# Strassen–Winograd block products of an attention kernel: from seven sums out of PSUM per block to five, with the weights' right half as first columns

## The chip, the cores and the metric

The kernel runs on one core of one Trainium2 chip. The metric is the device time of one execution in microseconds (us). The runs of the kernel before gave 1417.74, 1419.90 and 1419.27 us, median 1419.27 us. The engines are named as in the profile: PE (TensorE, matrix products), PEld (its weight loads), DVE (VectorE), ACT (ScalarE), POOL (GpSimd) and SP (SyncE, which issues nearly all DMAs here).

## The reference

There are 64 batches. `x` is 64 x 256 x 512, the context `c` is 64 x 256 x 384, all in fp32.

```python
text_p  = einsum('bld,dh->blh', x, W_text)  + b_text      # 512 -> 512
audio_p = einsum('bsd,dh->bsh', c, W_audio) + b_audio     # 384 -> 512
Q = layer_norm(text_p, g1, beta1);  K = layer_norm(audio_p, g2, beta2);  V = audio_p
alpha = softmax(einsum('blh,bsh->bls', Q, K) / sqrt(512))
h = einsum('bls,bsh->blh', alpha, V)
out = layer_norm(einsum('blh,hk->blk', h, W_out) + b_out + x, g_out, beta_out)
```

Since a softmax row sums to one, the kernel folds `W_audio` and `W_out` into one matrix `wao` and their biases into `bao`, and computes `alpha @ c @ wao + bao`.

## The kernel before

The order of the work is written out by hand: each engine runs its instructions in the order of the program text, and an instruction waits on semaphores for what it needs from the other engines. Tiles come from rotating pools. Of the 8 PSUM banks, six serve the pool `p_pj` (tag "pj"), two the pool `p_at` (scores, context, transposes). A new tile of a pool takes the bank of the tile six (or two) allocations earlier, and waits until that one has been read.

Three matrix products per batch are done by blocks: `q` (x times `W_text`), `k` (c times `W_audio`) and `y` (context times `wao`). Each has 256 rows and 512 columns of output, cut in 2 x 2 quarters of 128 rows by 256 columns, and is made of seven block products numbered 1 to 7 in place of eight (the Strassen–Winograd scheme). POOL adds up the operands beforehand (`weight_sums` and `weights_of_three` once per weight, `sum_x`, L304 to L307, and `sum_c`, L319 to L322, once per batch). A block product is one quarter of 128 x 256 fp32, half a PSUM bank. The method `products(...)` (L465 to L474) takes one bank for the one or two product numbers it is given and issues their matmuls (L472). The profile shows each fp32 matmul as two PE instructions, each called a pass here. One block of q has 28 passes (4 for each product), one of k or y has 22 (2 for products 1, 6 and 7, 4 for the rest).

The method `leave(n)` (L476 to L497, all instructions under L483) adds product n into the rows `qr`, `kr` or `yr` in SBUF, one DVE instruction for each number. Products 1, 6 and 7 go into two quarters (128 x 512, the product read twice by a broadcast), products 2, 5, 3 and 4 into one quarter (128 x 256). So there are seven DVE instructions for each block, and `rows` of the first 128 rows are complete after product 3, those of the second after product 4.

The program has a head (L743 to L853), a loop over 62 batches (L856 to L946) and an end (L949 to L1029).

- One pass of the loop holds on PE: scores of batch b (16 passes, L511), the q block of batch b+2 (28), the context of batch b-1 (12, L577), the k block of batch b+2 (22), and the y block of batch b-1 (22): 100 passes. On DVE it holds, in this order, the last three sums of an earlier y block, transposes of e, x and c squares (L91), the row maxima (L521), the q sums with the reciprocals (L538) between the first and the second of them, the transposes of q and k (L91, L439), the output's scaling (L694, L703), the k sums and the first four y sums.
- After its sums each q and k block goes this way: ACT squares the rows (L380), POOL makes the inverse deviation (L341, L343), ACT scales (L408), SP stores to DRAM (L418) and fetches squares of 32 x 32 in the next pass (L88), DVE transposes, ACT applies gamma and beta (L446), and the scores use the result.
- In the head, the first block product set of batch 1 is interleaved with other work. The lines that matter for q of batch 1 are, in program order:

```python
    part = bias_parts()                     # DVE, L231 and L233: four instructions
    q[1] = Blocks("q", 1, xs.pop(1), wt_blocks, bt_sb)
    q[1].products(1, 2)
    q[1].leave(1)
    q[0].turn()                             # DVE, L91
    q[0].affine(g1_sb, be1_sb)
    q[1].products(6, 5)
    q[1].leave(6)
```

- In the end, the y block of batch 61 (`last.o`) is interleaved likewise: `products(1, 2)`, the transpose of q of batch 63, `leave(1)`, `products(4)`, the transpose of k, `products(6, 5)`, and so on. It is followed on PE by the context of batch 62 and the scores of batch 63, and then by a chain of DVE, ACT and POOL work to the last store.

Of the kernel before, what the change touches and what calls it, by code (L numbers as in the profile page):

```python
# [9 lines left out]
F32 = mybir.dt.float32  # L10
# [5 lines left out]
P = 128  # L16
# [6 lines left out]
def kernel(  # L23
# [57 lines left out]
    p_pj = ctx.enter_context(tc.tile_pool(name="p_pj", bufs=6, space=PSUM))  # L81
# [24 lines left out]
    def load_squares(b):  # L106
        load_c(b)
        load_x(b)

    def load_rows(b):  # L110
        x_sb = xin.tile([P, LT, D], F32, tag="x", name=f"x_{b}")
        c_sb = cin.tile([P, ST, DA], F32, tag="c", name=f"c_{b}")
        nc.sync.dma_start(x_sb, x[b].rearrange("(t p) d -> p t d", p=P))
        nc.sync.dma_start(c_sb, c[b].rearrange("(t p) d -> p t d", p=P))
        return x_sb, c_sb
# [79 lines left out]
    class RowTurn:  # L195


        def __init__(self, rows_sb, chunks, name):
            self.rows, self.chunks = rows_sb, chunks
            tag = "yr" if chunks == DC else "kT"  # L200
            self.ar = work.tile([P, 2, chunks, P], F32, tag=tag, name=f"{name}r")
            self.T = work.tile([P, chunks, 2 * P], F32, tag=name, name=f"{name}_0")
# [81 lines left out]
    H2 = H // 2  # L284

    def weight_sums(w_sb, n, name):

        w = [[w_sb[:, j * n : (j + 1) * n, k * H2 : (k + 1) * H2] for k in (0, 1)] for j in (0, 1)]
        t = const.tile([P, 4, n, H2], F32, tag=name, name=name)
        add = nc.gpsimd.tensor_tensor  # L290
        add(t[:, 0], w[0][1], w[0][0], ALU.subtract)
        add(t[:, 1], w[1][1], t[:, 0], ALU.subtract)
        add(t[:, 2], w[1][1], w[0][1], ALU.subtract)  # L293
        add(t[:, 3], w[1][0], t[:, 1], ALU.subtract)
        ws = {1: w[0][0], 2: w[1][0], 3: w[1][1], 4: t[:, 3], 5: t[:, 0], 6: t[:, 1], 7: t[:, 2]}
        return {p: [ap[:, k, :] for k in range(n)] for p, ap in ws.items()}
# [31 lines left out]
    def weights_of_three(w_sb, name):  # L328

        ws = weight_sums(w_sb, 1, name)  # L330
        for n, k2 in ((2, 0), (3, 1), (5, 1), (4, 0)):
            ws[n].append(w_sb[:, 2, k2 * H2 : (k2 + 1) * H2])
        return ws

    def rstd_of(var, n, total=False):
# [118 lines left out]
    class Blocks(Projection):  # L454
# [3 lines left out]

        def __init__(self, name, b, sides, weights, bias):
            super().__init__(name, b, None, None, bias, None, 2)
            self.sides, self.weights = sides, weights

        def products(self, *ns):  # L465

            bank = p_pj.tile([P, 2, H2], F32, tag="pj", name=f"ps_{self.name}")
            for j, n in enumerate(ns):
                self.ps[n] = bank[:, j : j + 1, :]
                pairs = list(zip(self.sides[n], self.weights[n]))  # L470
                for i, (side, w) in enumerate(pairs):
                    nc.tensor.matmul(  # L472
                        bank[:, j, :], lhsT=side, rhs=w, start=(i == 0), stop=(i == len(pairs) - 1)
                    )  # L474

        def leave(self, n):  # L476

            both = self.ps.pop(n)
            one = both[:, 0, :]
            both = both.broadcast_to([P, 2, H2])  # L480
            c1, c2 = self.rows[:, 0, :], self.rows[:, 1, :]
            wide = lambda ap: ap.rearrange("p (k h) -> p k h", k=2)
            add = lambda o, i0, i1: nc.vector.tensor_tensor(o, i0, i1, ALU.add)  # L483
            if n == 1:
                add(wide(c1), both, wide(self.bias))
            elif n == 6:
                add(wide(c2), both, wide(c1))
            elif n == 2:
                add(c1[:, :H2], one, c1[:, :H2])
            elif n == 5:  # L490
                add(c2[:, H2:], one, c2[:, H2:])
            elif n == 3:
                add(c1[:, H2:], one, c2[:, H2:])
            elif n == 7:
                add(wide(c2), both, wide(c2))
            elif n == 4:
                add(c2[:, :H2], one, c2[:, :H2])  # L497

    class Attention:
        def __init__(self, b):  # L500
# [227 lines left out]
    def turn_next(b):  # L728
        xT[b] = turn_x(b)
        xs[b] = sum_x(xT.pop(b))  # L730
        cT[b] = turn_c(b)
        cs[b] = sum_c(cT.pop(b))
# [7 lines left out]
    q, k, xT, cT, rows = {}, {}, {}, {}, {0: (x_0, c_0)}  # L740
# [19 lines left out]
    k[0].evict(0)  # L760
    centre(wa_sb, mean_wa, AC)
    wa_blocks = weights_of_three(wa_sb, "wasum")
    for chunks in ([0, 1], [2, 3]):
        for t in range(LT):
# [15 lines left out]
    k[0].fetch()  # L780
    load_c(2)
    wt_blocks = weight_sums(wt_sb, DC // 2, "wtsum")
    q[0].evict(0)
    q[0].evict(1)
# [6 lines left out]
    q[0].fetch()  # L791
    xT[1] = turn_x(1)
    k[1] = Blocks("k", 1, cs.pop(1), wa_blocks, ba_sb)
    k[1].products(1, 2)
    k[1].leave(1)
    k[1].products(6, 5)
    k[1].leave(6)
    k[1].leave(2)
    k[1].leave(5)
    k[1].products(7, 3)  # L800
    k[1].leave(3)
    k[1].leave(7)
    k[1].products(4)
    k[1].leave(4)
    k[1].square()
    k[1].scales()
    xs = {1: sum_x(xT[1])}
# [21 lines left out]
    q[0].affine(g1_sb, be1_sb)  # L829
    q[1].products(6, 5)  # L830
    q[1].leave(6)
    q[1].leave(2)
    q[1].leave(5)
    q[1].products(7, 3)
    q[1].leave(3)
    q[1].leave(7)
    q[1].products(4)
    q[1].leave(4)
    q[1].square()
    q[1].scales()  # L840
    xT[2] = turn_x(2)
# [4 lines left out]
    fold_evict(2)  # L846
    bao_sb = fold_bias(part)
    wao_blocks = weights_of_three(wao_sb, "waosum")
    q[1].normalise()
    q[1].store()  # L850
# [4 lines left out]
    done = last = None  # L855
    for b in range(B - 2):  # L856
        three = b + 3 < B
        at = Attention(b)
        at.scores()
        if done:  # L860
            done.o.leave(3)
            done.o.leave(7)
            done.o.leave(4)
            done.add_x()
        if last:
            last.turn_e()
        if three and b:
            turn_next(b + 3)
        at.maxima()
        at.exponentials()  # L870
        if not b:
            k[1].turn()
        q2 = q[b + 2] = Blocks("q", b + 2, xs.pop(b + 2), wt_blocks, bt_sb)
        q2.products(1, 2)
        q2.leave(1)
        at.reciprocals()
        at.divide_e()
        if not b:
            k[1].affine(g2_sb, be2_sb)
        if b:  # L880
            q[b + 1].fetch()
            k[b + 1].fetch()
        at.store_e()
        if b + 4 < B:
            load_squares(b + 4)
        at.fetch_e()
        rows[b + 1] = load_rows(b + 1)
        if done:
            done.statistics()
        q2.products(6, 5)  # L890
        q2.leave(6)
        q2.leave(2)
        q2.leave(5)
        q2.products(7, 3)
        q2.leave(3)
        q2.leave(7)
        q2.products(4)
        q2.leave(4)
        q2.square()
        q2.scales()  # L900
        q[b + 1].turn()
        if not b:
            turn_next(3)
        if done:
            done.shift(0)
            done.shift(1)
        if last:
            last.context()
        q[b + 1].affine(g1_sb, be1_sb)
        if b:  # L910
            k[b + 1].turn()
            k[b + 1].affine(g2_sb, be2_sb)
        if done:
            done.settle(0)
            done.settle(1)
            done.store()
        q2.normalise()
        q2.store()
        if last:
            last.start_products()  # L920
        k2 = k[b + 2] = Blocks("k", b + 2, cs.pop(b + 2), wa_blocks, ba_sb)
        k2.products(1, 2)
        k2.leave(1)
        k2.products(6, 5)
        k2.leave(6)
        k2.leave(2)
        k2.leave(5)
        k2.products(7, 3)
        k2.leave(3)
        k2.leave(7)  # L930
        k2.products(4)
        k2.leave(4)
        k2.square()
        k2.scales()
        k2.normalise()
        k2.store()
        if last:
            last.o.products(1, 2)
            last.o.leave(1)
            last.o.products(6, 5)  # L940
            last.o.leave(6)
            last.o.leave(2)
            last.o.leave(5)
            last.o.products(7, 3)
            last.o.products(4)
        done, last = last, at  # L946


# [2 lines left out]
    k[B - 1].fetch()  # L951
    rows[B - 1] = load_rows(B - 1)
    at.scores()
    done.o.leave(3)
    done.o.leave(7)
    done.o.leave(4)
    done.add_x()
    add_bias(B - 2)
    last.turn_e()
# [16 lines left out]
    k[B - 1].turn()  # L976
    last.o.products(6, 5)
    last.o.leave(6)
    k[B - 1].affine(g2_sb, be2_sb)
    done.settle(0)  # L980
    last.o.leave(2)
    last.o.leave(5)
    last.o.products(7, 3)
    last.o.leave(3)
    last.o.leave(7)
    last.o.leave(4)
    last.add_x()
    at.context()
    done.settle(1)
# [72 lines left out]
```

## Time and profile before

| | |
|---|---|
| runs, median (lowest to highest) | 1419.27 us (1417.74 to 1419.90) |
| the profiled execution's own time | 1418.87 us |
| its span, first to last instruction | 1417.1 us |
| PE busy | 1404.4 us (99%), 6441 instructions |
| DVE busy | 1273.0 us (90%), 2134 instructions |
| ACT busy | 931.8 us (66%) |
| POOL busy | 878.0 us (62%) |
| granted PE clock, mean | 0.999 |

A line of the groups reads: line, engine, operation, output tile <- input tiles, shapes, count, then busy us in total and mean ns of one, then the idle time just before them with what ended it. The chain of waits is followed back from the last instruction: its pieces are the work or waits that set the end. A timeline line reads: start, us, engine, line, operation, tiles, count, and in brackets the idle time before with what ended it.

### The profile page before, as it was taken

Reading aid. Unit: us, or ns where it says so; the run is one execution under the profiler, and the core shown is the slowest. Engines: PE = TensorE matmul, PEld = TensorE weight load, DVE = VectorE, ACT = ScalarE, POOL = GpSimd, SP = SyncE. Lnnn points to the kernel's source line nnn. Section 1 sums busy time; section 2 is a strip of 40 time slices with the busy share of each in tenths; the row PEclk is TensorE's granted clock in tenths of the full one; section 3 lists DMA queues with packets and bytes.
Section 4 is the critical chain, followed back from the end, with each engine's and each line's share of the span. In section 5 each row is a group of like instructions: output and inputs, shape, how many; then the busy total and the mean of one; then the engine's idle time right before and its main releaser. Section 6 shows DMA issues by size and latency. Waiting matters only on the chain.

```text
span 1417.1 us, 23332 instructions
## 1 busy us (share of the span) xinstructions
PE 1404.4 (99%) x6441; PEld 1220.4 (86%) x6441; DVE 1273.0 (90%) x2134; ACT 931.8 (66%) x2293; POOL 878.0 (62%) x1295
## 2 busy tenths in 40 slices
PE   9999999999999999999999999999999999999997
PEld 5888888888888888888888888888888888888885
DVE  5789999999998999999999999999999999999988
ACT  4666676676676676765766766767667667667662
POOL 4556656666666666575566666665765666666645
PEclk9999999999999999999999999999999999999999
DMA  8898887888887788888878878887888788788763
GB/s 203 227 244 238 240 243 214 238 240 221 235 234 232 227 224 244 237 223 235 243 216 238 240 216 239 231 235 228 228 239 239 220 238 240 218 238 233 220 191 118
DMA packets 450583, 322.61 MB, mean 228 GB/s; under 512 B 154901, under 2 KB 382997, under 8 KB 450453
## 3 DMA queue, kind: packets, MB, share of 16 engines
q1 hardware_dynamic: 450356, 320.98, 79.9%
q8 instruction: 53, 0.87, 0.3%
q14 instruction: 78, 0.63, 0.2%
q10 hardware_dynamic: 96, 0.13, 0.0%
HBM read 204.09 MB, written 116.92 MB: 227 GB/s over the span
## 4 chain that ended last, share of the span: by engine, by line
PE 96%; DMA 1%; POOL 1%; DVE 1%; SPq 0%; issue 0%; ACT 0%; POOLq 0%; DVEq 0%; ACTq 0%
PE ps_q L472 27%; PE ps_y L472 21%; PE ps_k L472 21%; PE ps_sc L511 16%; PE ps_z L577 11%; DMA wt<-in_L_xattn_W_text_dram 1%; DMA xq<-in_x_dram 1%; POOL rstd L343 0%; PE ps_wao L245 0%; DVE st L267 0%; SPq L150 0%; POOL ve L341 0%; DVE y L632 0%; DVE y L698 0%; POOL wtsum L293 0%
## 5 line engine op out<-in xcount | busy, mean ns | idle before, releaser
L341 POOL TENSOR_SCALAR ve<-var 128x2 f32<-128x2 f32 x126 | 44.5, 353 | 305.9 <-ACT junk L380 305.9
L511 PE MATMUL ps_sc<-kT,qT 128*128 128x256 f32 x1024 | 231.5, 379 | 0.0
L528 ACT ACTIVATE e<-ps_sc,nmx 128x256 f32<-128x256 f32 x128 | 59.5, 469 | 246.4 <-DVE nmx L521 246.4
L483 DVE TENSOR_TENSOR qr<-ps_q,qr 128x512 f32<-128x512 f32 x378 | 188.0, 511 | 35.7 <-PE ps_q L472 24.0
L511 PEld LDWEIGHTS ps_sc<-kT,qT 128*128 128x128 f32 x1024 | 194.6, 190 | 26.9 <-ACT qT L446 0.2
L483 DVE TENSOR_TENSOR kr<-ps_k,kr 128x512 f32<-128x512 f32 x378 | 188.1, 511 | 24.3 <-PE ps_y L472 0.5
L483 DVE TENSOR_TENSOR yr<-ps_y,yr 128x512 f32<-128x512 f32 x372 | 185.1, 511 | 23.4
L593 POOL TENSOR_TENSOR yr<-yr,x 128x512 f32<-128x512 f32 x124 | 157.2, 1278 | 57.1 <-DVE yr L483 57.0
L577 PE MATMUL ps_z<-eT,c 128*128 128x256 f32 x768 | 176.5, 379 | 0.1
L472 PE MATMUL ps_q<-wtsum,xsum 128*128 128x256 f32 x756 | 173.6, 379 | 0.6 <-POOL xsum L305 0.6
L343 POOL TENSOR_TENSOR rstd<-ve,nhalf 128x2 f32<-128x2 f32 (+1 forms) x194 | 159.3, 821 | 16.2
L472 PE MATMUL ps_k<-wa,cT 128*128 128x256 f32 x630 | 166.8, 379 | 0.0
L472 PE MATMUL ps_y<-wao,zT 128*128 128x256 f32 x620 | 164.2, 379 | 0.0
L577 PEld LDWEIGHTS ps_z<-eT,c 128*128 128x128 f32 x768 | 145.8, 190 | 20.7 <-ACT e L528 0.5
L472 PEld LDWEIGHTS ps_q<-wtsum,xsum 128*128 128x128 f32 x756 | 143.6, 190 | 20.5 <-POOL xsum L305 1.0
L380 ACT ACTIVATE junk<-kr 128x512 f32<-128x512 f32 x126 | 79.3, 630 | 98.9 <-DVE kr L483 98.9
L446 ACT ACTIVATE qT<-qT,columns 128x256 f32<-128x256 f32 x256 | 132.8, 592 | 6.6 <-DVE qT L91 6.6
L472 PEld LDWEIGHTS ps_k<-wa,cT 128*128 128x128 f32 x630 | 119.6, 190 | 16.2
L446 ACT ACTIVATE kT<-kT,columns 128x256 f32<-128x256 f32 x256 | 132.1, 588 | 1.1 <-DVE kT L91 1.0
L472 PEld LDWEIGHTS ps_y<-wao,zT 128*128 128x128 f32 x620 | 117.7, 190 | 16.0
L408 ACT ACTIVATE kr<-kr,rstd 128x512 f32<-128x512 f32 x126 | 84.1, 714 | 70.7 <-POOL rstd L343 70.7
L703 DVE SCALAR_TENSOR_TENSOR yr<-yr,rstd,beo 128x512 f32<-128x512 f32 x124 | 127.5, 1066 | 0.6 <-POOL rstd L343 0.6
(150 smaller groups left out, 2945.9 us busy)
## 6 DMA issues: line engine op xcount, KB each, us to landing
kd<-kr SPq DMA_DIRECT2D x64, 512.0 KB, 3.1
kq<-kd SPq DMA_DIRECT2D x256, 128.0 KB, 3.4
qd<-qr SPq DMA_DIRECT2D x64, 512.0 KB, 5.5
qq<-qd SPq DMA_DIRECT2D x256, 128.0 KB, 3.3
xq<-in_x_dram SPq DMA_DIRECT2D x252, 128.0 KB, 2.9
x<-in_x_dram SPq DMA_DIRECT2D x63, 512.0 KB, 4.1
out_dram<-yr SPq DMA_DIRECT2D x62, 512.0 KB, 5.0
cq<-in_ctx_dram SPq DMA_DIRECT2D x252, 96.0 KB, 2.5
```

Source lines behind the costliest of these rows:

```text
L341: nc.gpsimd.tensor_scalar(ve, var, EPS, None, ALU.add)
L343: nc.gpsimd.tensor_tensor(r, ve, nhalf[:, :n], ALU.pow)
L380: nc.scalar.activation(junk, self.rows[:, t, :], AF.Square, scale=1.0 / math.sqrt(H), accum_out=self.var[:, t : t + 1],)
L408: nc.scalar.mul(row, row, self.r[t])
L446: nc.scalar.activation(self.T[:, k, :], self.T[:, k, :], AF.Identity, bias=bet[:, k : k + 1], scale=gam[:, k : k + 1],)
L472: nc.tensor.matmul(bank[:, j, :], lhsT=side, rhs=w, start=(i == 0), stop=(i == len(pairs) - 1))
L483: add = lambda o, i0, i1: nc.vector.tensor_tensor(o, i0, i1, ALU.add)
L511: nc.tensor.matmul(self.sc[:, t, :], lhsT=self.qT[:, k, bass.ts(t, P)], rhs=self.kT[:, k, :], start=(k == 0), stop=(k == HC - 1),)
L528: nc.scalar.activation(self.e[:, t, :], self.sc[:, t, :], AF.Exp, bias=self.nmx[:, t : t + 1], accum_out=self.den[:, t : t + 1],)
L577: nc.tensor.matmul(ps[:, j, :], lhsT=self.c_sb[:, s, bass.ts(lo + j, P)], rhs=self.eT[:, s, :], start=(s == 0), stop=(s == ST - 1),)
L593: nc.gpsimd.tensor_tensor(self.y[:, t, :], self.y[:, t, :], self.xb[:, t, :], ALU.add)
L703: nc.vector.scalar_tensor_tensor(self.y[:, t, :], self.y[:, t, :], self.r[t], beo_sb, ALU.mult, ALU.add)
```

## The change

The two column halves of the weights change roles: what the block scheme calls the first columns is now the right half of the weight. With that, products 2 and 5 belong to two quarters that are neighbours in the rows, and products 3 and 4 to the first and the last quarter, at one stride. Each of these two pairs shares a PSUM bank, and leaves it in one DVE instruction over 128 x 2 x 256. So a block has five sums (1, 6, 2+5, 3+4, 7), not seven. The banks are now by group, (1, 6), (2, 5), (3, 4) and (7), and `products` takes the bank of a group when the first of its products is issued. The order of the products in the loop becomes 1, 6, 2, 5, 3, 4, 7; the q block's sum of product 6 moves ahead of the reciprocals. In the head, `q[1].products(1, 2)` keeps its place, and so does `products(6, 5)` behind `q[1].leave(1)`; in the end the y block keeps `products(1, 2)`, `products(4)` and `products(6, 5)` in theirs. The instructions of ACT, POOL and SP keep their number, kind and order.

```diff
     def weight_sums(w_sb, n, name):
-        w = [[w_sb[:, j * n : (j + 1) * n, k * H2 : (k + 1) * H2] for k in (0, 1)] for j in (0, 1)]
+        w = [[w_sb[:, j * n : (j + 1) * n, k * H2 : (k + 1) * H2] for k in (1, 0)] for j in (0, 1)]
...
-            ws[n].append(w_sb[:, 2, k2 * H2 : (k2 + 1) * H2])
+            ws[n].append(w_sb[:, 2, (1 - k2) * H2 : (2 - k2) * H2])
...
         def products(self, *ns):
-            bank = p_pj.tile([P, 2, H2], F32, tag="pj", name=f"ps_{self.name}")
-            for j, n in enumerate(ns):
-                self.ps[n] = bank[:, j : j + 1, :]
+            for n in ns:
+                group = next(g for g in ((1, 6), (2, 5), (3, 4), (7,)) if n in g)
+                if group not in self.banks:
+                    self.banks[group] = p_pj.tile([P, 2, H2], F32, tag="pj", name=f"ps_{self.name}")
+                place = self.banks[group][:, group.index(n), :]
...
-        def leave(self, n):
...
+        def leave(self, *ns):
+            bank = self.banks[(1, 6) if ns[0] in (1, 6) else ns]
+            quarters = self.rows.rearrange("p t (k h) -> p (t k) h", k=2)
+            c1, c2 = quarters[:, :2], quarters[:, 2:]
...
+            elif ns == (2, 5):
+                add(quarters[:, 1:3], bank, quarters[:, 1:3])
+            elif ns == (3, 4):
+                add(quarters[:, 0:4:3], bank, c2)
...
         if not b:
             k[1].turn()
         q2 = q[b + 2] = Blocks("q", b + 2, xs.pop(b + 2), wt_blocks, bt_sb)
-        q2.products(1, 2)
+        q2.products(1, 6)
         q2.leave(1)
+        q2.leave(6)
         at.reciprocals()
...
-        q2.products(6, 5)
-        q2.leave(6)
-        q2.leave(2)
-        q2.leave(5)
-        q2.products(7, 3)
-        q2.leave(3)
+        q2.products(2, 5)
+        q2.leave(2, 5)
+        q2.products(3, 4)
+        q2.leave(3, 4)
+        q2.products(7)
         q2.leave(7)
-        q2.products(4)
-        q2.leave(4)
...
     q[1].products(6, 5)
     q[1].leave(6)
-    q[1].leave(2)
-    q[1].leave(5)
-    q[1].products(7, 3)
-    q[1].leave(3)
+    q[1].leave(2, 5)
+    q[1].products(3, 4)
+    q[1].leave(3, 4)
+    q[1].products(7)
     q[1].leave(7)
-    q[1].products(4)
-    q[1].leave(4)
...
     last.o.products(6, 5)
     last.o.leave(6)
+    last.o.leave(2, 5)
     k[B - 1].affine(g2_sb, be2_sb)
     done.settle(0)
-    last.o.leave(2)
-    last.o.leave(5)
-    last.o.products(7, 3)
-    last.o.leave(3)
+    last.o.products(3)
+    last.o.leave(3, 4)
+    last.o.products(7)
     last.o.leave(7)
-    last.o.leave(4)
```

## The prediction

> **What bounds the kernel now.** I read four views: the busy shares on the page, the waits by engine, the chain of waits, and the order of DVE's work where PE stops.
>
> Waits of PE, with engine and line waited for, us in total, times, longest:
>
> ```profile
> PE ps_ones L193 <- POOL ones L122: 1.5, 1, 1.5
> PE ps_y L472 <- DVE kr L483: 1.4, 1, 1.4
> PE ps_q L472 <- POOL xsum L305: 0.6, 1, 0.6
> ```
>
> PE is 99% busy, and these are its longest waits, each of which occurs once. None belongs to a steady loop pass. From there on PE runs its 100 passes in 21.58 us, pass after pass, without a gap (712.46 to 734.04 us between the starts of two q blocks: 215.8 ns each). The loop goes at PE's pace, and time can only come or go where PE waits: in the head and in the end.
>
> The chain of waits in the head (start, us, work):
>
> ```profile
> 36.17 0.74 POOL xsum L305
> 36.92 0.04 issue
> 36.96 4.58 PE ps_q L472 x20
> 41.54 3.43 PE ps_wao L245 x8
> ...
> 76.92 2.60 PE ps_y L472 x12
> 79.52 0.04 issue
> 79.56 0.70 DVE kr L483
> 80.27 0.02 issue
> 80.29 0.44 DVE kr L483
> 80.72 0.14 issue
> 80.86 2.40 PE ps_y L472 x10
> 83.25 3.45 PE ps_sc L511 x16
> ```
>
> At 36.96 the matmuls of q[1]'s product 6 start, as soon as POOL has their operand. All later pieces are PE's, back to back, until 79.52. There the third bank of the first y block is the first bank of the k block before it, and PE waits until DVE's third k sum has read it (80.29 to 80.72).
>
> DVE's timeline at the places where a first sum lies between two products, in the head and in the end:
>
> ```profile
> 36.31 0.88 DVE L231 TENSOR_SCALAR part<-wo,columns 128x512 f32<-128x512 f32 x1
> 37.22 3.02 DVE L233 SCALAR_TENSOR_TENSOR part<-wo,columns,part 128x512 f32<-128x512 f32 x3
> 40.16 0.68 DVE L483 TENSOR_TENSOR qr<-ps_q,bt 128x512 f32<-128x512 f32 x1
> ...
> 1385.81 1.25 DVE L91 STREAM_TRANSPOSE qT<-qq 128x1024 f32<-128x1024 f32 x1 [0.41 <-DMA qq<-qd]
> 1386.98 0.65 DVE L483 TENSOR_TENSOR yr<-ps_y,bao 128x512 f32<-128x512 f32 x1
> ```
>
> The sum of product 1 runs late in both: at 40.16, behind the bias parts, and at 1386.98, behind a transpose.
>
> **Fewer sums.** Groups of DVE by form (count, then busy us and mean ns):
>
> ```profile
> L483 DVE TENSOR_TENSOR qr<-ps_q,qr 128x256 f32<-128x256 f32 x252 | 100.9, 421 | 23.5 <-PE ps_q L472 14.2
> L483 DVE TENSOR_TENSOR qr<-ps_q,qr 128x512 f32<-128x512 f32 x126 | 87.1, 691 | 12.2 <-PE ps_q L472 9.8
> ```
>
> Four sums of 421 ns become two of 691 ns (taking the row for 512 elements; the stride of 3+4 has no row): 1684 - 1382 = 302 ns less per block. With 63 q, 63 k and 62 y blocks that is 57 us of DVE. On the path it is worth nothing: what hides it is PE's unbroken row of passes, 21.58 us against 19.8 us of DVE in a pass. If that cover were gone, up to 57 us would show.
>
> **The order 1, 6, 2, 5, 3, 4, 7 and the moved sum.** The operands of product 6 are there: zsum's second step ends at 723.5, and y needs it at 726.3. Nothing is paid. In q, the sum of product 6 (0.69) now stands ahead of the reciprocals, where DVE idled 0.49 us for ACT. The reciprocal comes some 0.25 us later, and behind it ACT's division, SP's store of e and SP's loads queued after it. e returns for a transpose in the next pass that does not wait for DMA. Price nothing; if that cover is gone, 0.25 x 62 = 15 us.
>
> **The wait at 79.52 gets shorter or goes.** The first k bank now holds 1 and 6 and is free after the second sum, 0.46 us earlier (80.25, not 80.71). The wait cost 83.25 - 76.92 - 4.75 = 1.58 us (a y block without it takes 4.75).
>
> **A new wait in the head.** q[1]'s products 1 and 6 now share a bank, and between them stands `leave(1)`. The changed program's list of waits says it: the first matmul of product 6 waits for the DVE instruction that sums product 1. Before, 6 lay in another bank. ACT, POOL and SP are unchanged, and DVE reaches that sum by the same instructions, so it ends at 40.84 again. With the 0.14 us from a sum's end to PE's start (80.72 to 80.86), product 6 starts at 40.98, not at 36.96: +4.02 us. Queued behind it on PE is all the rest, and the chain from 36.96 to 79.52 has no slack. A lower bound: two of the three L233 instructions took 1.10 us beside POOL, the third 0.75; were all like the third, +3.3.
>
> How much comes back? PE now reaches the place of the old wait at 83.54. The k sums there follow a chain of row maxima, sums, scaling, store and fetch. Part of it moves with PE, part was waiting for DMA. Following it, I get the second k sum done between 80.6 and 82.5: the old wait is gone, -1.58. If all moved by 4.02, only the 0.46 came back. So the head costs 4.02 - 1.58 = 2.44, at most 3.56. Later batches repeat the loop without a wait.
>
> **A new wait in the end.** The same occurs in y of batch 61: product 6 started at 1387.11, and the sum of product 1 ends at 1387.63; +0.14 for the start and +0.1 for the restart (after a wait the second pass comes 0.3 us after the first, not 0.2): +0.76. The transpose ahead of that sum waited 0.41 us for DMA; the k and q sums before its fetch now end some 0.4 us earlier, which may remove as much: +0.35. I take 0.5. It is on the path: the last scores follow on PE without a gap, and the row maxima at 1395.94 wait for them. The shorter y sums between gain nothing there.
>
> **Sum.** The profiled execution took 1418.87 us (span 1417.1 and 1.8 around it): 1418.87 + 2.44 + 0.5 = 1421.8. The median of the runs lies 0.40 above the profiled execution: 1422.2. That is +0.21%. About 0.2%, 2.84 us, is what a measurement of this kernel can tell from no change, so "slower" and "same" meet nearly at my number.
>
> **A rule against it.** PE's last pass before the new wait starts at 36.00, so it stands idle for about 4.7 us. In this trace PE waits of 1.35 us leave the clock at 1.00, and after the last matmul at the end of the program (1409.4) the windows show 1.00 until 1414.5 and 0.59 for 1414.5 to 1415: it falls 5.2 us after. By these rows 4.7 us is just under it. If the clock did fall: at the start, passes of 128 columns stand 213 ns apart from 1.5 to 4.9 us and 110 ns after, 3.3 us at half rate, a loss of at most 1.7.
>
> The Trainium skill, "TensorE: Matmul & The Clock Gate" (Part 1), states that the clock falls to half after an idle window of some 3.4 us, windows that run free of the program. By that rule the idle stretch can catch a whole window in some executions and not in others; with the loss above, such an execution would take 1423.9 us.
>
> **Rivals.**
> - *The clock falls in the new gap*: +1.1 to +1.7 more, 1423.3 to 1423.9. For: the length of the gap. Against: the 5.2 us at the end.
> - *Not slower: the old wait and the head's other chains take the new wait up.* What bound PE at 79.52 was a chain through DMA and DVE, so a head that is late on PE could find room behind it. This decides only if PE has over 4 us of waits after 41 us; the trace shows 1.58. What speaks for it is that batch 1's own fetches were waiting for DMA. Result: 1418.0 to 1419.7.
> - *DVE's 57 us show*, if the loop hung on DVE: 1362 to 1375. Against: DVE idles each pass, PE never.
> - *A wait in each loop pass*, by the moved sum or a bank: from 0.1 us a pass it is +6, with 0.25 it is +15: 1428 to 1437. Against: banks are free over 1.5 us ahead (k's second sum ends at 726.6, y's third bank is needed at 728.43).
>
> **Chances.** Forecast (1421.0 to 1423.0) 0.62; clock 0.20; taken up 0.08; DVE 0.03; loop wait 0.07. The forecast splits at 1422.1, the bound: 0.33 slower, 0.29 same. The clock case is slower but for 0.01, the loop wait slower, "taken up" same, DVE faster but for 0.01. Sum: slower 0.59, same 0.39, faster 0.02. The range reaches from 1420.0 (between "taken up" and the forecast, with the lower bounds of +3.3 and +0.35) to 1424.8 (the clock case with the upper bound of the wait in the end and part of the 3.56).
>
> **What would show it.** Right: a PE wait at `ps_q` for DVE `qr` of about 4.6 us near 41 us, a short one at `ps_y` for DVE `yr` near 1390 us, none for `kr`; DVE busy about 1216 us; a loop pass still 21.58 us; the page's clock slices near 41 us tell whether it fell. Wrong: a loop pass other than 21.58 us, or a product 6 that starts before its neighbour's sum has ended.

## The result, and the profile after

| | before | after |
|---|---|---|
| runs, median (lowest to highest) | 1419.27 us (1417.74 to 1421.16), 9 runs | 1423.60 us (1423.23 to 1425.29), 9 runs |
| the profiled execution and its span | 1418.87, 1417.1 us | 1425.29, 1423.5 us |
| mean granted PE clock | 0.999 | 0.996 |
| DVE busy | 1273.0 us | 1232.9 us |

The ratio is 1.0031 [1.0023, 1.0040]: slower by 0.3%, and the predicted 1422.2 us was 1.4 us short. The profiled execution after is the slowest of its nine, 1.7 us above their median; its head is already 0.9 us late at the first block product on PE, ahead of which no PE instruction was changed (first pass of k[1] at 23.69 us against 22.76, of q[1] at 35.42 against 34.49).

PE's waits after, in the columns of the prediction:

```profile
PE ps_q L478 <- DVE qr L490: 4.7, 1, 4.7
PE ps_ones L193 <- POOL ones L122: 1.5, 1, 1.5
```

The forecast wait is there, the old one on `kr` is gone. The chain of waits after, in the head and around the first y block:

```profile
37.31 0.87 DVE part L231
...
41.22 0.61 DVE qr L490
41.83 0.14 issue
41.96 7.34 PE ps_q L478 x20
...
84.67 4.75 PE ps_y L478 x22
```

The chain now runs through the bias parts and the sum of product 1, and the y block has its bare 4.75 us. But the 20 passes of q[1] behind the wait take 7.34 us where they took 4.58. The windows view shows why (start and end of the stretch, its length, busy us of PE, PEld, DVE, ACT and POOL with their instructions, granted clock, DMA share, GB/s):

```profile
33.95:37.36 3.41, 3.36 (x13) 1.96 (x11) 1.53 (x5) 2.45 (x8) 1.82 (x4) 1.00 0.91 266
37.36:40.78 3.42, 0.00 (x0) 0.00 (x0) 3.31 (x4) 3.32 (x7) 2.52 (x3) 1.00 0.91 227
40.78:44.19 3.41, 2.23 (x5) 1.85 (x6) 2.42 (x4) 0.21 (x1) 0.00 (x0) 0.50 0.92 272
44.19:47.60 3.41, 3.41 (x9) 2.70 (x8) 1.24 (x2) 1.87 (x4) 0.00 (x0) 0.50 1.05 249
47.60:51.02 3.42, 3.42 (x13) 2.25 (x12) 2.37 (x3) 1.44 (x4) 0.14 (x1) 1.00 0.85 163
```

The borders of these stretches are those at which the granted clock changes. In this trace its changes lie a whole number of steps of 3.413 us apart: two from the fall at 40.78 to the rise at 47.60, and 404 from 40.78 to the next fall at 1419.77, behind the last matmul. Such a stretch is called a window below.

The granted clock is 0.50 for two windows, from 40.78 to 47.60. PE works 2.23 + 3.41 us of them at half rate, which costs half of that, 2.8 us (7.34 - 4.58 = 2.76). This is the rival "the clock falls", with a larger loss than its 1.7.

The loop after, two scores blocks of the chain:

```profile
715.34 3.45 PE ps_sc L517 x16
...
736.92 3.45 PE ps_sc L517 x16
```

They are 21.58 us apart, as before. Between the scores of batch 2 and of batch 60 lie 1251.83 us in both traces: nothing in the loop moved the time.

The end, DVE's transpose and sum and PE's passes of product 6 (both from the timelines):

```profile
1391.51 1.23 DVE L91 STREAM_TRANSPOSE qT<-qq 128x1024 f32<-128x1024 f32 x1
1392.67 0.65 DVE L490 TENSOR_TENSOR yr<-ps_y,bao 128x512 f32<-128x512 f32 x1
1393.46 1.10 PE L478 MATMUL ps_y<-waosum,zsum 128*128 128x256 f32 x4
```

The transpose has no idle time before it any more, and product 6 starts 0.14 us after the sum; with the restart (1.10 us for its four passes, not 1.03) it costs 0.26 us.

The two traces add up. Start of the head +0.93, wait +4.07 and clock +2.76 (these two together, from the transpose `ps_v` to the third `wao` product, 13.83 us against 7.00), old wait -1.59 (scores of batch 0 to those of batch 2, 35.83 against 37.42), end +0.26: 6.43, against 1425.29 - 1418.87 = 6.42.

### The profile page after: what moved, and what is told of

It reads as the page before. It is cut to its first block, busy times and chain, and to the rows that moved or that the text cites. A ratio compares the mean times of both kernels' runs of the same rounds, so it can differ in the third digit from the quotient of the medians.

```text
span 1423.5 us, 22648 instructions
## 1 busy us (share of the span) xinstructions
PE 1407.9 (99%) x6441; PEld 1223.2 (86%) x6441; DVE 1232.9 (87%) x1758; ACT 932.8 (66%) x2293; POOL 875.9 (62%) x1295
## 4 chain that ended last, share of the span: by engine, by line
PE 97%; DVE 1%; DMA 1%; POOL 0%; issue 0%; ACT 0%; POOLq 0%; SPq 0%; DVEq 0%
PE ps_q L478 27%; PE ps_k L478 21%; PE ps_y L478 21%; PE ps_sc L517 16%; PE ps_z L583 11%; PE ps_wao L245 1%; PE ps_q L365 1%; DMA c<-in_ctx_dram 0%; DVE part L233 0%; DMA wa<-in_L_xattn_W_audio_dram 0%; PE ps_k L365 0%; DVE st L267 0%; DVE y L638 0%; POOL ve L344 0%; POOL rstd L346 0%
## 5 line engine op out<-in xcount | busy, mean ns | idle before, releaser
L490 DVE TENSOR_TENSOR qr<-ps_q,qr 128x512 f32<-128x512 f32 x252 | 174.2, 691 | 93.9 <-PE ps_q L478 91.5
L478 PE MATMUL ps_q<-wtsum,xsum 128*128 128x256 f32 x756 | 195.7, 382 | 4.7 <-DVE qr L490 4.7
L490 DVE TENSOR_TENSOR kr<-ps_k,kr 128x512 f32<-128x512 f32 x252 | 174.3, 692 | 22.5 <-DVE kr L490 0.9
L490 DVE TENSOR_TENSOR yr<-ps_y,yr 128x512 f32<-128x512 f32 x248 | 171.5, 692 | 22.0 <-DVE yr L490 0.9
L478 PE MATMUL ps_k<-wa,cT 128*128 128x256 f32 x630 | 177.1, 379 | 0.0
L478 PE MATMUL ps_y<-wao,zT 128*128 128x256 f32 x620 | 174.1, 379 | 0.0
L709 DVE SCALAR_TENSOR_TENSOR yr<-yr,rstd,beo 128x512 f32<-128x512 f32 x124 | 128.7, 1075 | 0.6 <-POOL rstd L346 0.6
```

The costliest lines, as they stand in the source:

```text
L478: nc.tensor.matmul(place, lhsT=side, rhs=w, start=(i == 0), stop=(i == len(pairs) - 1))
L709: nc.vector.scalar_tensor_tensor(self.y[:, t, :], self.y[:, t, :], self.r[t], beo_sb, ALU.mult, ALU.add)
```

## The experiments

The times below are medians; "before" is the kernel before, run on the same chip beside them (1419.03 us in the first four, 1418.88 in the next four, 1418.58 in the last three). Theory: the whole loss is a shared bank in the head (a wait of 4.07, and the clock that falls in it) and in the end (0.26), less the old wait; the five sums are worth nothing. Rivals: the reordering or the sums cost something in the loop; the saved DVE time counts; the 2.76 us are no matter of the clock.

| kernel | median us (runs) | ratio to before, interval |
|---|---|---|
| e1_head | 1418.60 (10) | 0.9997 [0.9988, 1.0007] |
| e3_dummy | 1421.74 (10) | 1.0022 [1.0013, 1.0032] |
| e4_parts | 1418.68 (10) | 1.0002 [0.9992, 1.0011] |
| e6_alone | 1423.91 (5) | 1.0036 [1.0023, 1.0049] |
| e9_best | 1417.96 (11) | 0.9993 [0.9984, 1.0002] |
| e5_seven | 1424.24 (5) | 1.0035 [1.0022, 1.0048] |
| e7_half | 1420.45 (10) | 1.0013 [1.0004, 1.0022] |
| e11_three | 1422.83 (7) | 1.0028 [1.0017, 1.0038] |
| e12_six | 1423.45 (5) | 1.0039 [1.0024, 1.0053] |
| e13_again | 1419.72 (1) | |
| e8_recip | 1424.69 (1) | |

**Both products of the bank ahead of the sum (e1_head).**

```diff
-    q[1].products(1, 2)
+    q[1].products(1, 6)
     q[1].leave(1)
...
-    q[1].products(6, 5)
+    q[1].products(2, 5)
```

> Changed kernel with one edit in the head: q of batch 1 issues products 1 and 6 ahead of the sum of product 1, and products 2 and 5 where 6 and 5 stood. Theory (PE waits for the sum in the bank that products 1 and 6 share, and its clock falls while it waits): no wait of PE for DVE qr over 1 us, clock 1.00 from 30 to 50 us, time 1417.5 to 1418.5 us. Rival (the loss lies in the loop or in the wider sums): time stays at 1423 to 1424. Rival without the clock: the profile of the changed kernel lost 4.1 us alone to the wait, so about 1419.5.

Measured 1418.60. PE's wait for DVE is gone; product 6 is asked for four passes earlier and waits for its operand instead, and the 24 passes behind that wait come at 5.45 / 24 = 0.23 us each:

```profile
PE ps_q L478 <- POOL xsum L308: 0.9, 1, 0.9
```

```profile
36.45 5.45 PE ps_q L478 x24
```

So the order of two products against one sum decides the loss: at the median nothing of it is left (ratio 0.9997, interval 0.9988 to 1.0007).

**Other work for PE in the same wait (e3_dummy).** Twenty extra matmuls of ones into another bank; product 6 still has to wait for the sum.

```diff
     q[1].products(1, 2)
+    ps_d = p_at.tile([P, P], F32, tag="at", name="ps_d")
+    for _ in range(20):
+        nc.tensor.matmul(ps_d, lhsT=ones, rhs=ones, start=True, stop=True)
     q[1].leave(1)
```

> Changed kernel with 20 matmuls of ones (40 passes of 0.11 us, 4.4 us, into a bank that nothing else needs then) issued on PE between products 2 and 6 of q of batch 1, so that PE is busy while product 6 waits for the sum. Theory: product 6 starts as late as before, but its passes are 0.216 us apart, not 0.427; the clock stays at 1.00; time 1421.0 to 1422.3 us. Rival (the wait alone costs the time, the clock nothing): 1423.6 as the changed kernel.

Measured 1421.74, clock 0.998 to 0.999. PE has no wait for DVE now; two pieces of its chain:

```profile
36.41 4.46 PE ps_d L833 x40
40.87 4.49 PE ps_q L478 x20
```

Product 6 starts at 40.87 us, as late as forecast (40.98), but its 20 passes take 4.49 us, not 7.34. Work that nobody needs made the kernel 1.9 us faster at the median than the changed one (1.6 with each against its own kernel before). So the 2.76 us of the changed kernel's trace are the clock's, and the waits by themselves are worth 1421.74 - 1419.03 = 2.7 us, where the forecast's sum had 2.44 + 0.5.

**The sum ahead of the bias parts (e4_parts).** DVE makes the sum of product 1 first; the bank stays shared.

```diff
-    part = bias_parts()
     q[1] = Blocks("q", 1, xs.pop(1), wt_blocks, bt_sb)
     q[1].products(1, 2)
     q[1].leave(1)
+    part = bias_parts()
```

> Changed kernel with DVE's four bias parts moved behind the sum of product 1 of q of batch 1; the banks and the order of PE stay. Theory: the sum ends by about 37.9 us, product 6 starts within 1 us of it being possible before, the clock stays at 1.00, time 1417.5 to 1419.0 us. Rival (sharing a bank costs time whenever, or the loss lies in the loop): 1422 to 1424.

Measured 1418.68. PE waits 0.8 us, for POOL alone. The shared bank is harmless when its first sum is early.

**The shared banks alone, with seven sums (e6_alone).** The kernel before, in which only q[1]'s products 1 and 6 (and 2 and 5) share banks.

```diff
-    q[1].products(1, 2)
+    q[1].split_products(1, 2)      # 1 into bank A, 2 into bank B
     q[1].leave(1)
...
-    q[1].products(6, 5)
+    q[1].split_products(6, 5)      # 6 into bank A, 5 into bank B
```

> The kernel before with one edit: in q of batch 1 alone, product 6 goes into the bank of product 1 and product 5 into that of product 2; seven sums, order and everything else as before. Theory: the whole loss is there: a wait of PE for DVE qr of over 4 us near 41 us, half the clock behind it, time 1422.5 to 1424.5 us. Rival (the loss lies in the loop or in the wider sums): 1419.3, as the kernel before.

Measured 1423.91, the changed kernel's time with the kernel before's seven sums. Waits, then the chain:

```profile
PE ps_q L475 <- DVE qr L497: 4.4, 1, 4.4
```

```profile
41.22 3.75 PE ps_q L475 x8
44.97 3.29 PE ps_q L486 x12
```

The 20 passes take 7.04 us. Here too the old wait on `kr` is gone, though this kernel's banks for k and y are those of before: it went because PE came later, not because the bank came free earlier. Its windows:

```profile
36.01:39.43 3.42, 0.79 (x4) 0.36 (x2) 3.35 (x6) 3.42 (x8) 2.29 (x3) 1.00 0.94 221
39.43:42.84 3.41, 1.62 (x4) 1.39 (x5) 2.67 (x4) 0.15 (x1) 0.00 (x0) 0.50 0.96 284
42.84:46.25 3.41, 3.41 (x9) 2.69 (x9) 1.62 (x4) 2.08 (x4) 0.00 (x0) 0.50 0.97 250
```

The clock fell after a window in which PE had worked 0.79 of 3.41 us: it need not be idle as a whole.

**Seven sums in the changed kernel (e5_seven).**

```diff
-                add(quarters[:, 1:3], bank, quarters[:, 1:3])
+                add(quarters[:, 1], bank[:, 0], quarters[:, 1])
+                add(quarters[:, 2], bank[:, 1], quarters[:, 2])
```

and 3+4 likewise.

> The changed kernel with its banks and its order of products, but the pairs 2+5 and 3+4 leave PSUM in two instructions each, so seven sums again. Theory (the fewer sums are worth nothing, since the loop goes at PE's pace): 1423.6 us as the changed kernel, 1422.8 to 1424.6, with DVE busier by 35 to 60 us than the 1232.9 of the changed kernel. Rival (part of the saved DVE time reached the end of the program and softened the loss): from 1426 up to 1480.

Measured 1424.24, as the changed kernel. DVE's busy time rose by only 24 us, outside the expected 35 to 60 (here the 252 small sums of q take 95.3 us, in the kernel before 100.9, at 420 and 421 ns each, so more of them overlap), but none of it shows: fewer sums are worth nothing here. In the changed kernel DVE waits for PE instead (the sums of q, idle time last):

```profile
L490 DVE TENSOR_TENSOR qr<-ps_q,qr 128x512 f32<-128x512 f32 x252 | 174.2, 691 | 93.9 <-PE ps_q L478 91.5
```

Before, its two groups had 23.5 + 12.2 us of idle time.

**A shorter wait (e7_half, e11_three).** Two of the four bias parts, or one, go behind the sum of product 1.

```diff
-    part = bias_parts()
+    part = bias_parts(0, 2)            # e11_three: (0, 3)
...
     q[1].leave(1)
+    bias_parts(2, HC, part)            # e11_three: (3, HC, part)
```

> The changed kernel with two of the four bias parts on DVE moved behind the first sum of q of batch 1, so that this sum ends some 2.0 us earlier and PE stands idle for about 2.7 us, not 4.7. Theory (the wait costs what it is long, and the clock falls only if a whole window of some 3.4 us is idle): a wait of about 2.0 to 2.2, the clock 0.999, 1419.3 + 2.1 + 0.3 - 1.6 = 1420.1, between 1419.4 and 1420.7. Rival (any wait of some us lowers the clock): two cold windows more, 1422.5 to 1423.

> The changed kernel with one of the four bias parts moved behind the first sum of q of batch 1: PE stands idle for about 3.7 us. Theory A (the windows have a fixed place, in the changed kernel 37.4 to 40.8 us, and the clock falls only where one is idle as a whole): in most executions PE is back before 40.8, the clock stays at 0.999, 1419.3 + 3.1 + 0.3 - 1.6 = 1421.1, between 1420.4 and 1421.8; an execution that is 0.9 us late at the head, as the profiled one of the changed kernel was, may still fall. Theory B (any idle time longer than 3.4 us lowers the clock): 1421.1 + 2.8 = 1423.9, clock 0.997 in every run. Theory C (the fall comes some 4 us after the last pass): as A, in every run.

e7_half: 1420.45. Six runs took 1420.04 to 1420.56 at a mean clock of 0.998, four 1421.18 to 1421.79 at 0.997. The profiled one is of the six; it waits 2.8 us:

```profile
34.55:37.96 3.41, 2.15 (x10) 1.44 (x8) 2.71 (x6) 2.95 (x7) 3.33 (x5) 1.00 0.97 254
37.96:41.38 3.42, 1.89 (x9) 1.72 (x10) 2.79 (x4) 1.47 (x3) 0.23 (x1) 1.00 1.03 270
```

The wait is split by a window's border, PE is busy for more than half of both, and the clock stays. In the four others it probably fell; no trace shows one of them.

e11_three: 1422.83, between the two theories' times and right for neither. It waits 3.6 us, and its windows show both the fall and why it came late:

```profile
34.79:38.20 3.41, 2.00 (x10) 1.44 (x8) 2.85 (x6) 3.08 (x7) 3.33 (x5) 1.00 0.94 257
38.20:41.62 3.42, 1.22 (x6) 1.12 (x7) 2.67 (x4) 1.36 (x3) 0.12 (x1) 1.00 0.95 288
41.62:45.03 3.41, 3.41 (x10) 2.70 (x9) 2.51 (x3) 2.07 (x4) 0.00 (x0) 0.50 0.85 193
```

PE is back at 40.40 and works at full clock for 1.22 us; then the clock falls under it, because the window that ends at 41.62 was too empty. One cold window, busy throughout, costs 1.7 us: 20 passes in 6.24 us. None of the three theories on record fits. Windows have no fixed place in the program (they lie 0.8 us later than in the changed kernel), no idle window of 3.4 us is needed, and PE's return 3.6 us after its last pass did not prevent the fall. Theory B had the fall right in every run (0.996 to 0.998) but priced it at 2.8 us; its limit of 3.4 us of idle time is refuted by the next run, not by this one.

**A wait shorter than a window (e12_six).** As e3_dummy with six extra matmuls, so that PE stands idle for 3.2 us, less than any whole window.

```diff
-    for _ in range(20):
+    for _ in range(6):
```

> The changed kernel with six matmuls of ones (twelve passes, some 1.3 us) ahead of the waiting product 6, so that the wait keeps its end but PE stands idle for only about 3.3 us of it, less than one clock window (3.41 us). Theory (the clock falls after a window in which PE was busy for less than some 0.4 of the time; windows with 0.00, 0.23, 0.31 and 0.36 brought the fall, those with 0.48 and more did not): the place of the windows differs from run to run, so the fall comes in most runs, about 7 to 9 of 10, at 1422.6 to 1424 us and clock 0.996 to 0.998, and the rest take 1421.7. Rival (a whole window must be idle): no run falls, 1421.4 to 1422.0, clock 0.999 throughout.

Measured 1423.45, every run at 0.996 to 0.997. The profiled run:

```profile
37.44:40.85 3.41, 0.47 (x5) 0.27 (x3) 3.31 (x5) 2.00 (x5) 0.77 (x1) 1.00 1.01 265
40.85:44.26 3.41, 3.18 (x8) 2.58 (x9) 2.02 (x3) 1.58 (x4) 0.00 (x0) 0.50 0.89 249
44.26:47.68 3.42, 3.42 (x16) 2.83 (x15) 1.82 (x3) 1.07 (x4) 0.00 (x0) 1.00 1.09 238
```

This settles it against the rival: PE's wait was 3.2 us, no window was idle as a whole, and the clock fell. By the clock it fell in all five runs, where 7 to 9 of 10 were expected, and two of them took longer (1424.33 and 1425.14) than the expected 1424. With one cold window the loss is 1.54 us (6.12 against 4.58 for the 20 passes).

**The sum of product 6 behind the reciprocals again (e8_recip).**

```diff
         q2.leave(1)
-        q2.leave(6)
         at.reciprocals()
+        q2.leave(6)
```

> The changed kernel with the sum of product 6 of q back behind the reciprocals in the loop. Theory (the moved sum costs nothing, since PE never waits in the loop): 1423.6 us as the changed kernel, 1422.8 to 1425.3, with 1251.83 us from the scores of batch 2 to those of batch 60 as there. Rival (the moved sum costs time in each pass): shorter by 0.1 us a pass or more, so at least 6 us.

One run, 1424.69, the loop (scores of batch 2 to those of batch 60) again 1251.83 us: the moved sum is free.

**The kernel before, profiled again (e13_again).**

> The kernel before, unchanged, profiled once more: how steady is its wait of 1.58 us at the first y block? If it is steady, the first y block lasts 6.2 to 6.4 us and the way from its scores of batch 0 to those of batch 2 is 37.4 us again; if it depends on when DMAs land, 36.3 to 37.2, and then the term of 1.58 us is too large for the median run, which would agree with the gain of the variants without waits, 0.4 to 0.9 us at the median where their traces sum to 1.0 to 1.8.

```profile
PE ps_y L472 <- DVE kr L483: 1.8, 1, 1.8
```

1.4 in the first trace, 1.8 in this one, and 37.86 us from the scores of batch 0 to those of batch 2, against 37.42: the old wait isn't steady, but this trace moves it up, not down as I had supposed. Why the variants without waits gain less at the median than in their traces stays open.

**Both waits taken out (e9_best).** PE's order in the head as in the kernel before; in the end, product 6 ahead of the sum.

```diff
     q[1].products(1, 2)
+    q[1].products(6, 5)
     q[1].leave(1)
     q[0].turn()
     q[0].affine(g1_sb, be1_sb)
-    q[1].products(6, 5)
     q[1].leave(6)
...
-    last.o.leave(1)
     last.o.products(4)
+    last.o.products(6)
+    last.o.leave(1)
     q[B - 1].affine(g1_sb, be1_sb)
     k[B - 1].turn()
-    last.o.products(6, 5)
+    last.o.products(5)
```

> The changed kernel with products 6 and 5 of q of batch 1 issued on PE before the sum of product 1 (so that PE's order is that of the kernel before, and neither the sum nor POOL is waited for out of turn), and with product 6 of y of batch 61 issued ahead of that block's first sum. Theory (the loss is a wait at each of the two places, plus the clock that falls in the first): both waits and the fall are gone, and only the removed wait on kr (1.58 us) is left of the change: 1419.3 - 1.6 = 1417.7, between 1417.0 and 1418.4, faster than the kernel before; the granted clock 0.999 again; no PE wait on qr or yr. Rival (the five sums or the new order of the loop cost something of their own that the first experiment, 1418.6, hid): 1418.6 or more.

Measured 1417.96, inside the expected range, and 0.9 us below the kernel before, where 1.6 was expected; its interval still holds 1. Its chain:

```profile
36.65 4.58 PE ps_q L478 x20
...
76.61 4.84 PE ps_y L478 x22
```

Nothing is left of the wait in the head, and hardly anything of the old one (4.84 us for a block that takes 4.75 without it). It is 5.6 us faster than the changed kernel's median (5.2 with each against its own kernel before); that it beats the kernel before is likely, not shown.

## Why the prediction was right, and where it was wrong

The measured 1423.60 lies in the range of 1420.0 to 1424.8, but not by the forecast case (1421.0 to 1423.0, chance 0.62). It lies there because the range was drawn to take in the clock case, which had 0.20. The sum itself had the waits right to some 0.3 us each and put the clock at nothing.

- **Fewer sums worth nothing: right.** The loop is equal to 0.01 us, and e5_seven pays nothing for seven. DVE's saving was mis-sized, 40 us for 57: the page's busy total counts neighbouring sums that overlap once (252 sums of 421 ns are 106 us, the row says 100.9), so the row's total divided by its count, 400 ns, was the price.
- **The moved sum, free: right** (e8_recip).
- **The old wait: right in size** (-1.58 forecast, -1.59 measured). The second k sum ended at about 85.1 us, later than the forecast 80.6 to 82.5, but PE came to the place at 87.26, not at 83.54. PE's lateness alone removes the wait (e6_alone). In e1_head PE is only 0.35 us later there than before, and yet the wait is gone: the second k sum ends at 79.0, 1.7 us before the 80.72 at which the kernel before had its bank free. The changed order explains 0.46 of that. Whether DVE's shorter chain of sums or other times of the DMAs made the rest, no run separates, so outside the loop the five sums may be worth something.
- **The new wait in the head: right** (+4.02 against 4.07; e6_alone makes it by itself, e4_parts removes it). The Trainium skill, "PSUM — Partial Sum Buffer" (PSUM bank collisions raise a hardware error), gives the reason for waiting on a bank rather than on an address: two engines at one bank, in the same partitions, collide even in different columns. The traces show the wait; no run here lets two engines collide.
- **The wait in the end:** +0.26 for 0.5, below its lower bound of 0.35. The earlier transpose that the bound allowed for did happen.
- **The clock: wrong, and this is the step that failed.** "By these rows 4.7 us is just under it" took the 5.2 us between the last matmul and the fall at the end of the program for a delay. The windows of that place in the kernel before, cut where the clock changes, read otherwise:

```profile
1407.77:1411.18 3.41, 1.64 (x8) 1.10 (x6) 3.24 (x8) 0.00 (x0) 1.33 (x2) 1.00 0.41 154
1411.18:1414.59 3.41, 0.00 (x0) 0.00 (x0) 2.71 (x6) 0.00 (x0) 1.70 (x2) 1.00 0.19 70
1414.59:1417.00 2.41, 0.00 (x0) 0.00 (x0) 0.00 (x0) 0.00 (x0) 0.00 (x0) 0.50 0.35 118
```

The last matmul ended in a window that was busy enough (1.64 of 3.41 us); the next one was empty, and the fall came at its end. The 5.2 us are the rest of one window and one whole window. They are no delay: at the end of e9_best the fall comes 2.2 us after the last matmul (1407.60 to 1409.78), behind a window with 1.23 us of work. A gap of 4.65 us, wherever the borders lie, leaves some window with at most 3.41 - 4.65/2 = 1.1 us of work, and each full-clock window seen with 1.22 us or less brought the fall. By this working the case that got a chance of 0.20 was all but certain; all nine runs show 0.996 or 0.997.
- **Its price: mis-sized.** "A loss of at most 1.7" is one cold window. In the changed kernel's profiled run the first cold window, 2.23 of 3.41 us busy, did not restore the clock, and a second followed: 2.76. The rival's 1423.3 to 1423.9 nevertheless holds the median of 1423.60, since the other runs lost less than the profiled one: 1.7 us less in all, of which 0.9 is its late head. That the rest is windows that lie otherwise, as e12_six with its 1.54 suggests, is argued, not shown.
- **The rule that was weighed against the row:** the Trainium skill, "TensorE: Matmul & The Clock Gate" (Part 1), spoke of windows of some 3.4 us that run free of the program, and was the better guide: steps of 3.41 us, with borders that differ from run to run, are in every trace. It asks for an idle window, though, and here windows with 0.47, 0.79 and 1.22 us of work were enough.
- **The other rivals** are out: nothing took the wait up, DVE's time did not show, no loop pass waits.

## What to carry to other kernels

Two products whose sums leave PSUM at different times should not share a bank when one is issued behind the other's sum: group banks by when they are read, or issue both products first. When PE is the bound, freeing another engine buys nothing, and one wait of a few us costs its length and, where it leaves a clock window too empty, the clock as well. To price such a gap, cut the trace into the clock's own windows, place the gap badly, and ask how much work the emptiest window keeps; a delay read off one place is no threshold.

## What was not expected of the hardware

- The clock goes by how full a window was. Full-clock windows with 0.00, 0.47, 0.79 and 1.22 us of work out of 3.41 brought the fall, those with 1.41 (the end of e13_again), 1.64, 1.89 and 2.00 did not. Cold windows in which PE was busy at half rate for 1.62, 2.23 and 2.73 us (the last in e8_recip) did not restore it, those with 3.18 and 3.41 did. One bound on the work done, about 0.4 of what a window can hold at full clock, would just fit all of these (2.73 us at half rate are 1.37 us of work, and 1.41 kept the clock); it was not tried by itself.
- The clock can fall while PE is at work (e11_three: 1.2 us after PE's return).
- In e8_recip, where 0.7 us of DVE work moved in each pass, other instructions took other times: POOL's 128x256 step of `zsum` went from 1164 to 737 ns, DVE's last scaling of `yr` from 1075 to 960 ns, POOL's busy time from 875.9 to 839.2 us. Which instructions of DVE and POOL then ran side by side was not followed. Off the critical path it moved no time.
